# The last step of a recurrence: kept rows raised and loaded early, scale in the matrix, first turns on other banks

## The chip, the core and the metric

One core of a Trainium2 chip runs the whole program. The metric is device time in microseconds of one execution, the median of the runs shown; a profile of one execution comes with it. TensorE (PE) multiplies matrices; VectorE (DVE), ScalarE (ACT) and GpSimd (POOL) work on elements; SyncE (SP) issues transfers. In the profile PEld is TensorE's weight load, which overlaps its products.

## What is computed

Two layers, each a graph attention over 3327 nodes of 256 features and a feed-forward part. This document is about the end of layer 1: a layer norm, thirty steps of a small recurrence, and a residual.

```python
def step(h, _):
    h = h + 0.01 * jnp.tanh(h)
    h = h * jax.nn.sigmoid(h)
    h = _layernorm(h, ln_w, ln_b)
    h = jnp.einsum('bsc,dc->bsd', h, W) + b
    return (h, None)
x, _ = jax.lax.scan(step, x, None, length=N_ITERS)      # 30 steps
...
x = x + _L1_gnn_ref(_layernorm(x, axis=-1), adj, L1_gnn_W, L1_gnn_a)
x = x + _L1_ffn_ref((_layernorm(x, axis=-1))[None], L1_ffn_ln_w, L1_ffn_ln_b, L1_ffn_W, L1_ffn_b)[0]
```

The `x` of the last line's sum is needed thirty steps after it was last touched.

## The kernel before

The rows are 26 tiles of 128, held in SBUF as `x`. Layer 1's attention (`attend`) ends tile by tile; `begin_state` (L1070) writes the finished rows to `kept` in DRAM (L1072) and then normalizes `x` in place, times S = 100. So the recurrence's state lies in `x`, scaled by S, and the rows for the residual lie in `kept`.

`recurrence_parameters` (L845) prepares the step: `wc` is the weight matrix with the norm's weight in it, without its column mean, times S; `bb` is the bias, times S. `fb` holds the bias as loaded, over all partitions.

The 26 tiles form seven groups, six of four tiles and one of two. A number `at` runs over all groups of all steps: group `at % 7` of step `at // 7`, with `LAST` = 210. Each group goes through `tanh` (ACT, L1112), `add` (POOL, L1115), `silu` (ACT, L1119), `measure` (VectorE, L1124 and L1127), `invert` (POOL, L1132: the inverse deviation `rr`), a transposition, `product` (TensorE, L1181) and `evict` (VectorE, L1191: `x = po * rr + bb`). Transposition is done in one of two ways. Groups 1 and 3 (and group 0 of the first step) are turned on TensorE (`turn_here`, L1145) into PSUM banks, and ACT or VectorE copies them out (L1148). Groups 0, 2, 4, 5 and 6 go by DMA: ACT splits the words into halves (L1156), SP sends them to DRAM (`send_away`, L1158) and fetches them back transposed (`take_back`, L1168). The received tiles lie in slices of the space that held the adjacency matrix, which is why the profile calls them `adjT`.

The order is written out by hand. One loop over `at` calls the stages of different groups: tanh for group at + 6, invert for at + 1, send for at + 4, add for at + 5, product and evict for at, measure for at + 3, take_back or turn for at + 3. From the second step on (for TensorE from the third turn on) `keep_in_program_order` holds every engine's queue, SP's too, to that order. The earlier instructions, among them the first two groups' turns, are placed by a scheduler in between those of the attention before them.

PSUM has eight banks. Layer 1 uses two for single banks (`ps`) and six for its accumulators (`ps_o`, read at L1064 and L1065); the recurrence keeps `ps` and puts two more single banks (`ps_t`) and two double ones for its products where the six were. `turn_here` takes its banks from `ps` and `ps_t` by turns, `ps` first.

In the last step `evict` does more: it loads the group's rows from `kept` (L1198, on SP's queue, two buffers), adds them to 1/S times the result (L1199) and stores the sum through `move_pairs` (L74, SP's queue, L77). The last two tiles hold 255 rows; their store is three transfers, of 112 rows of pairs, 15 and a single row.

Of the kernel before, what the change touches and what calls it, by code (L numbers as in the profile page):

```python
# [11 lines left out]
F32 = mybir.dt.float32  # L12
# [5 lines left out]
ALU = mybir.AluOpType  # L18
# [3 lines left out]
P = 128  # L22
ALPHA = 0.2
EPS = 1e-5
N_STEPS = 30
S = 100.0
G = 4
# [4 lines left out]
def gat_moe_gat_recurrent_ffn(ctx: ExitStack, tc: tile.TileContext, a: dict, out: bass.AP):  # L32
    nc = tc.nc
    N, D = a["x"].shape
    KD = D // P
# [9 lines left out]
    groups = [range(t, min(t + G, NT)) for t in range(0, NT, G)]  # L45
# [9 lines left out]
    def spread(n):  # L55

        cut = n - n % 16
        return [r for r in ((0, cut), (cut, n)) if r[0] < r[1]]
# [14 lines left out]

    def move_pairs(dram, tile, c0, c1, into_dram):  # L74

        def move(dst, src):
            nc.sync.dma_start(*((dst, src) if into_dram else (src, dst)))  # L77

        full = min(c1, PAIRS - 1)
        if full > c0:  # L80
            move(
                dram[c0 * 2 * P : full * 2 * P, :].rearrange("(t p b) d -> p t (b d)", p=P, b=2),
                tile[:, : 2 * (full - c0), :].rearrange("p (t b) d -> p t (b d)", b=2),
            )
        if c1 == PAIRS:
            base, last = (PAIRS - 1) * 2 * P, 2 * (PAIRS - 1 - c0)
            for r0, r1 in spread(REST // 2):
                move(
                    dram[base + 2 * r0 : base + 2 * r1, :].rearrange("(p b) d -> p (b d)", b=2),
                    tile[r0:r1, last : last + 2, :].rearrange("p b d -> p (b d)"),  # L90
                )
            if REST % 2:
                move(dram[base + REST - 1 : base + REST, :], tile[REST // 2 : REST // 2 + 1, last, :])
# [262 lines left out]
    fb = rec.tile([P, D], F32, name="fb")  # L356
# [26 lines left out]
    with ExitStack() as moe:  # L383
# [21 lines left out]
        ps = moe.enter_context(tc.tile_pool(name="ps0", bufs=4, space=PSUM))  # L405
# [3 lines left out]
        def bank():  # L409
            return ps.tile([P, 512], F32, name="bank")  # L410
# [242 lines left out]
        for s0, n in ((0, FIRST), (FIRST, ALWAYS - FIRST)):  # L653
            no = 0
            for lane in range(SETS):
                here = two[:, 0, s0 + lane : s0 + n : SETS]
# [124 lines left out]
        def put(s, room, behind):  # L781
            planes = room.bitcast(I16)
            with tc.issue_after(behind):
                nc.scalar.copy(
                    planes.rearrange("p (b d) -> p b d", b=2),
                    gotten.pop(s).bitcast(I16).rearrange("p (d b) -> p b d", b=2),
                )
            put_down[s] = next(asked)
            nc.gpsimd.dma_start(put_down[s], planes)
# [55 lines left out]
        def recurrence_parameters(bank):  # L845


            pb = bank()[:, :D]
            for k in range(KD):
                nc.tensor.matmul(  # L850
                    pb, lhsT=lb[:, k : k + 1].to_broadcast([P, P]), rhs=fW[:, k, :], start=(k == 0), stop=(k == KD - 1)
                )
            nc.vector.tensor_tensor(bb, pb, fb, ALU.add)
            nc.vector.tensor_scalar(bb, bb, S, None, op0=ALU.mult)
            pc = bank()[:, :D]
            for k in range(KD):
                nc.vector.tensor_scalar(wc[:, k, :], fW[:, k, :], lw[:, k : k + 1], None, op0=ALU.mult)
                nc.tensor.matmul(pc, lhsT=ones_r, rhs=wc[:, k, :], start=(k == 0), stop=(k == KD - 1))
            for k in range(KD):
                nc.vector.scalar_tensor_tensor(wc[:, k, :], pc, -1.0 / D, wc[:, k, :], op0=ALU.mult, op1=ALU.add)  # L860
                nc.vector.tensor_scalar(wc[:, k, :], wc[:, k, :], S, None, op0=ALU.mult)
# [118 lines left out]
        wc = rec.tile([P, KD, D], F32, name="wc")  # L980
        bb = rec.tile([P, D], F32, name="bb")
# [18 lines left out]
    kept = dram.tile([NP, D], F32, name="kept")  # L1000
# [8 lines left out]
    ps = ctx.enter_context(tc.tile_pool(name="ps2", bufs=2, space=PSUM))  # L1009
# [72 lines left out]

    with ExitStack() as st:
        ps_t = st.enter_context(tc.tile_pool(name="ps3t", bufs=2, space=PSUM))
        turns = cycle((ps, ps_t))
        ps_o = st.enter_context(tc.tile_pool(name="ps3o", bufs=2, space=PSUM))
        last_p = st.enter_context(tc.tile_pool(name="last", bufs=2))

        apart = cycle([dram.tile([G * P, 2, D], I16, name=f"apart{q}") for q in range(4)])
        space = graph.tile([P, PAIRS, NP], BF16, name="adjT").rearrange("p c n -> p (c n)").bitcast(F32)  # L1090
        spaces = [space[:, i * G * D : (i + 1) * G * D] for i in range(8)]
        room_parts, room_back = cycle(spaces[:3]), cycle(spaces[3:])

        AWAY = (0, 2, 4, 5, 6)
        COUNT = len(groups)
        LAST = N_STEPS * COUNT

        class Group:

            def __init__(self, at):  # L1100
                self.at = at
                self.ts = groups[at % COUNT]
                self.n = len(self.ts)
                self.hs = x[:, self.ts[0] : self.ts[0] + self.n, :]
                self.away = at % COUNT in AWAY and at > 1

            def put(self, ins):
                return tc.keep_in_program_order(ins) if self.at >= COUNT else ins

# [25 lines left out]
                )  # L1135

            def turn_here(self):
                pool = next(turns)
                zT = steps["zT"].tile([P, G, KD, P], F32, name="zT")
                for c in range(self.n // 2):  # L1140
                    pt = pool.tile([P, 2, KD, P], F32, name="bank")
                    for j in range(2):
                        for k in range(KD):
                            (tc.keep_in_program_order if self.at > 1 else lambda ins: ins)(
                                nc.tensor.transpose(pt[:, j, k, :], self.z[:, 2 * c + j, k * P : (k + 1) * P], ident)  # L1145
                            )
                    copied = nc.vector.tensor_copy if (self.at % COUNT, c) == (3, 0) else nc.scalar.copy
                    self.put(copied(zT[:, 2 * c : 2 * c + 2, :, :], pt))  # L1148
                self.zT = lambda j, k: zT[:, j, k, :]
# [26 lines left out]
            def product(self):  # L1176
                self.po = ps_o.tile([P, G, D], F32, name="po")
                for j in range(self.n):
                    for k in range(KD):
                        tc.keep_in_program_order(  # L1180
                            nc.tensor.matmul(  # L1181
                                self.po[:, j, :], lhsT=self.zT(j, k), rhs=wc[:, k, :],
                                start=(k == 0), stop=(k == KD - 1),
                            )
                        )

            def evict(self):
                ts, n = self.ts, self.n
                for j in range(n):
                    self.put(  # L1190
                        nc.vector.scalar_tensor_tensor(  # L1191
                            self.hs[:, j, :], self.po[:, j, :], self.r[:, j : j + 1], bb, op0=ALU.mult, op1=ALU.add
                        )
                    )
                if self.at >= LAST - COUNT:
                    here = slice(ts[0] * P, (ts[-1] + 1) * P)
                    old = last_p.tile([P, G, D], F32, name="old")
                    nc.sync.dma_start(old[:, :n, :], kept[here, :].rearrange("(t p) d -> p t d", p=P))  # L1198
                    nc.vector.scalar_tensor_tensor(  # L1199
                        self.hs, self.hs, 1.0 / S, old[:, :n, :], op0=ALU.mult, op1=ALU.add  # L1200
                    )
                    move_pairs(out, self.hs, ts[0] // 2, (ts[-1] + 1) // 2, True)

        live = {}

        def on(at, *what):
            if 0 <= at < LAST:
                if at not in live:
                    live[at] = Group(at)
                for w in what:  # L1210
                    w(live[at])

        for at in range(-6, LAST):
            on(at + 6, Group.tanh)
            on(at + 1, Group.invert)
            on(at + 4, lambda g: g.away and g.send_away())
            on(at + 5, Group.add)
            on(at, Group.product, Group.evict)
            on(at + 3, Group.measure)
            on(at + 3, lambda g: g.away and g.take_back())  # L1220
            on(at + 5, Group.silu)
            on(at + 3, lambda g: g.away or g.turn_here())
            live.pop(at, None)
# [49 lines left out]
```

## Time and profile before

| | |
|---|---|
| median of 3 runs | 1819.82 us (1819.78 to 1823.14) |
| the profiled execution | 1820.76 us |
| its span, first to last instruction | 1819.0 us |
| mean granted TensorE clock | 0.995 |
| busy: PE, DVE, ACT, POOL | 1764.8, 1303.0, 1214.2, 916.2 us |
| recurrence (L1181): TensorE's products | 2144 on tiles by DMA, 976 on turned ones (each product counts as two) |
| one step in the middle | 24.2 us |

A row of the timeline reads: start and duration in us, engine, line, operation, output from input, how many, and in brackets the idle time before it with what ended it. The waits list who waited for whom, with the sum in us, the count and the longest. The table by stretch gives for each interval its length and the busy time of each engine with the number of instructions, then the granted clock (1.00 is full), the mean busy share of the DMA engines and GB/s. The landing of a transfer is read from the events of its semaphore in the trace.

### The profile page before, as it was taken

The page shows a single profiled execution, that of the slowest core. Times are in us where ns is not written, and L with a number is a line of the kernel's source. Part 1 is how long each engine was busy: PE and PEld are TensorE (multiplying, and loading weights), DVE is VectorE, ACT ScalarE, POOL GpSimd, SP SyncE. Part 2 cuts the span into 40 slices and gives each one's busy share as a digit, 9 for nine tenths or more (in the row PEclk, how much of TensorE's full clock was granted, in tenths as well). Part 3 has the DMA queues.
Part 4 walks back from the last instruction along what each step waited for, and adds up shares of the span by engine and source line. Part 5 has one row for each costly group of instructions (what it writes and reads, how often), then busy time and mean ns, then how long its engine had stood idle before and what let it go on. Part 6 is the DMA issues. An engine that isn't in the chain of part 4 may idle for free.

```text
span 1819.0 us, 32184 instructions
## 1 busy us (share of the span) xinstructions
PE 1764.8 (97%) x10768; PEld 1608.8 (88%) x10768; DVE 1303.0 (72%) x3861; ACT 1214.2 (67%) x1557; POOL 916.2 (50%) x702
## 2 busy tenths in 40 slices
PE   6999999999999999799999999999999999999997
PEld 6999999899999999688888878888888888888885
DVE  7888888863222222657677678889899988998997
ACT  2877677642212121456666579999999999999993
POOL 3011212155454542101111028999999999999993
PEclk9999999999999999899999999999999999999999
DMA  8996360247796875400000038888877888878778
GB/s 174 121 126 81 78 102 10 72 161 211 239 257 192 212 205 163 154 14 18 18 21 16 12 103 188 199 195 199 198 198 192 194 194 196 198 198 201 196 191 233
DMA packets 497026, 269.75 MB, mean 148 GB/s; under 512 B 361797, under 2 KB 469116, under 8 KB 496858
## 3 DMA queue, kind: packets, MB, share of 16 engines
q1 hardware_dynamic: 478722, 229.29, 50.6%
q0 software_dynamic: 13456, 33.60, 10.7%
q10 hardware_dynamic: 4680, 4.76, 0.8%
q8 instruction: 88, 1.44, 0.3%
q14 instruction: 80, 0.66, 0.1%
HBM read 168.19 MB, written 105.58 MB: 151 GB/s over the span
## 4 chain that ended last, share of the span: by engine, by line
PE 54%; DVE 3%; DMA 1%; issue 0%; ACT 0%; SPq 0%; POOL 0%; ACTq 0%; DVEq 0%; POOLq 0%
PE po L1181 36%; PE acc L286 15%; PE bank L1145 3%; DVE pT L281 1%; PE acc L163 1%; DMA old<-kept 1%; DVE x L1030 0%; DMA given<-wh,to 0%; DMA zT<-given 0%; DVE x L1199 0%; DVE x L1191 0%; DVE st L116 0%; POOL rstd L121 0%; DVE low L1064 0%; SPq L1168 0%
## 5 line engine op out<-in xcount | busy, mean ns | idle before, releaser
L276 ACT ACTIVATE e<-rb,minus,full 128x384 f32<-128x384 f32 (+3 forms) x494 | 399.3, 823 | 167.4 <-DVE pT L281 149.6
L1181 PE MATMUL po<-wc,adjT 128*128 128x256 f32 x2144 | 480.0, 380 | 7.5 <-DMA adjT<-apart 5.5
L1115 POOL TENSOR_TENSOR th<-th,x 128x1024 f32<-128x1024 f32 (+1 forms) x210 | 464.7, 2213 | 17.4 <-ACT th L1112 15.7
L281 DVE SCALAR_TENSOR_TENSOR pT<-e,part,adjT 128x384 f32<-128x384 f32 (+3 forms) x494 | 383.5, 782 | 118.4 <-PE acc L286 102.4
L1181 PEld LDWEIGHTS po<-wc,adjT 128*128 128x128 f32 x2144 | 405.9, 191 | 63.5 <-issue 4.9
L1191 DVE SCALAR_TENSOR_TENSOR x<-po,rr,bb 128x256 f32<-128x256 f32 x780 | 323.7, 476 | 73.4 <-PE po L1181 72.8
L286 PE MATMUL acc<-wh,pT 128*128 128x129 f32 x2704 | 310.4, 276 | 2.1 <-DVE pT L281 2.1
L286 PEld LDWEIGHTS acc<-wh,pT 128*128 128x128 f32 x2704 | 305.3, 192 | 2.9 <-DVE pT L281 2.7
L286 PE MATMUL acc<-s_wh,pT 128*128 128x257 f32 x1352 | 295.5, 381 | 4.0 <-DVE pT L281 4.0
L286 PEld LDWEIGHTS acc<-s_wh,pT 128*128 128x128 f32 x1352 | 255.8, 190 | 43.1 <-DVE pT L281 7.4
L1124 DVE BATCH_NORM_STATS2 stats<-z 128x6 f32<-128x256 f32 x780 | 274.4, 412 | 1.4 <-ACT z L1119 1.4
L1156 ACT COPY adjT<-z 128x1024 int16<-128x1024 int16 x268 | 266.9, 1039 | 2.1 <-DVE pT L281 2.0
L1132 POOL TENSOR_TENSOR rr<-v,neg_half 128x4 f32<-128x4 f32 (+1 forms) x210 | 205.6, 979 | 94.2 <-DVE v L1127 88.9
L121 POOL TENSOR_TENSOR rstd<-ve,neg_half 128x4 f32<-128x4 f32 (+3 forms) x28 | 31.9, 1141 | 409.4 <-DVE ve L119 325.6
L1112 ACT ACTIVATE th<-x 128x1024 f32<-128x1024 f32 (+1 forms) x210 | 208.8, 994 | 41.5 <-DVE x L1191 37.7
L1181 PE MATMUL po<-wc,zT 128*128 128x256 f32 x976 | 220.8, 379 | 0.1
L1119 ACT ACTIVATE z<-th 128x1024 f32<-128x1024 f32 (+1 forms) x210 | 209.0, 995 | 6.5 <-POOL th L1115 6.4
L1181 PEld LDWEIGHTS po<-wc,zT 128*128 128x128 f32 x976 | 182.9, 190 | 24.0 <-DVE x L1191 0.5
L931 ACT ACTIVATE e<-bank 128x512 f32<-128x512 f32 x61 | 36.4, 597 | 239.0 <-issue 184.8
L939 DVE TENSOR_TENSOR pT<-e,bank 128x512 f32<-128x512 f32 x61 | 41.9, 687 | 180.3 <-PE bank L881 160.1
L903 POOL DMA_INDIRECT given<-wh,to x61 | 61.1, 1001 | 114.5 <-DVE wh L902 100.0
L594 POOL DMA_INDIRECT lists<-pair,ati x52 | 63.1, 1214 | 107.8 <-DVE ati L581 50.0
(204 smaller groups left out, 1648.0 us busy)
## 6 DMA issues: line engine op xcount, KB each, us to landing
apart<-adjT SPq DMA_DIRECT2D x268, 256.0 KB
wh<-in_w_dram SPq DMA_DIRECT2D x120, 512.0 KB
first_set<-in_w_dram SPq DMA_DIRECT2D x63, 512.0 KB
in_bytes<-in_adj_dram POOLq DMA_DIRECT2D x3, 2496.0 KB
asked<-e POOLq DMA_DIRECT2D x42, 128.0 KB
adjT<-apart SPq DMA_TRANSPOSE x268
x<-in_x_dram SPq DMA_DIRECT2D x6, 512.0 KB
kept<-x SPq DMA_DIRECT2D x8, 384.0 KB
```

Of the source, the lines that this page charges most:

```text
L276: nc.scalar.activation(e[:, : n * P], rb[:, : n * P], AF.Relu, scale=sc.full[:, j, h : h + 1], bias=sc.minus[:, j, h : h + 1],)
L281: masked = nc.vector.scalar_tensor_tensor(pT[:, : n * P], e[:, : n * P], sc.part[:, j, h : h + 1], adjT[:, j // 2, ts[0] * P : (ts[-1] + 1 ...
L286: nc.tensor.matmul(po[c], lhsT=pT[:, c * P : (c + 1) * P], rhs=wh[:, j, h, :], start=(j == 0 and c % per_bank == 0), stop=(j == NT - 1), s ...
L594: put = nc.gpsimd.indirect_dma_start(out=lists, out_offset=bass.IndirectOffsetOnAxis(ap=ati[: rows(t), s, j : j + 1], axis=0), in_=pair[: ...
L1112: self.put(nc.scalar.activation(self.th, self.hs, AF.Tanh, scale=1.0 / S))
L1115: self.put(nc.gpsimd.tensor_tensor(self.th, self.th, self.hs, ALU.add))
L1119: self.put(nc.scalar.activation(self.z, self.th, AF.Silu, scale=1.0 / S))
L1124: self.put(nc.vector.bn_stats(stats[:, j, :6], self.z[:, j, :]))
L1132: nc.gpsimd.tensor_tensor(self.r[:, : self.n], self.v[:, : self.n, 1], neg_half[:, : self.n], ALU.pow)
L1156: self.put(nc.scalar.copy(parts[:, c : c + 2], halves[:, c : c + 2]))
L1181: nc.tensor.matmul(self.po[:, j, :], lhsT=self.zT(j, k), rhs=wc[:, k, :], start=(k == 0), stop=(k == KD - 1),)
L1191: nc.vector.scalar_tensor_tensor(self.hs[:, j, :], self.po[:, j, :], self.r[:, j : j + 1], bb, op0=ALU.mult, op1=ALU.add)
```

## The change

The kept rows get the bias added while they lie in DRAM: seven accumulating DMAs from GpSimd (`raise_old`), one for each group, after the product and eviction of group g in step 2 + 2g. Seven loads on SP's queue (`load_old`) bring the raised rows into SBUF, that of group g in step 16 + g, into seven slices of the old adjacency space. A second matrix `wc_last` = `wc` / S is made with the first load, and the last step's products use it. The last step's eviction is then `x = po * rr + old` and nothing more. For stores `move_pairs` takes SP's and ACT's queue by turns, beginning with SP in each call. The bias without S now stays in `fb`. The first two turns take their banks from `ps`, later ones from `ps_t` and `ps` by turns.

```diff
     def move_pairs(dram, tile, c0, c1, into_dram):
+        queues = cycle((nc.sync, nc.scalar) if into_dram else (nc.sync,))
         def move(dst, src):
-            nc.sync.dma_start(*((dst, src) if into_dram else (src, dst)))
+            next(queues).dma_start(*((dst, src) if into_dram else (src, dst)))
...
-            nc.vector.tensor_tensor(bb, pb, fb, ALU.add)
-            nc.vector.tensor_scalar(bb, bb, S, None, op0=ALU.mult)
+            nc.vector.tensor_tensor(fb, pb, fb, ALU.add)
+            nc.vector.tensor_scalar(bb, fb, S, None, op0=ALU.mult)
...
-        turns = cycle((ps, ps_t))
+        turns = cycle((ps_t, ps))
-        last_p = st.enter_context(tc.tile_pool(name="last", bufs=2))
...
+        wc_last = spaces[8][:, : KD * D].rearrange("p (k d) -> p k d", k=KD)
+        olds = [
+            spaces[9 + i].rearrange("p (t d) -> p t d", d=D)[:, : len(ts), :] for i, ts in enumerate(groups)
+        ]
...
             def turn_here(self):
-                pool = next(turns)
+                pool = next(turns) if self.at > 1 else ps
...
-                                self.po[:, j, :], lhsT=self.zT(j, k), rhs=wc[:, k, :],
+                                self.po[:, j, :], lhsT=self.zT(j, k), rhs=(wc if self.at < LAST - COUNT else wc_last)[:, k, :],
...
-                            self.hs[:, j, :], self.po[:, j, :], self.r[:, j : j + 1], bb, op0=ALU.mult, op1=ALU.add
+                            self.hs[:, j, :], self.po[:, j, :], self.r[:, j : j + 1],
+                            olds[self.at % COUNT][:, j, :] if last else bb, op0=ALU.mult, op1=ALU.add,
                         )
                     )
-                if self.at >= LAST - COUNT:
-                    here = slice(ts[0] * P, (ts[-1] + 1) * P)
-                    old = last_p.tile([P, G, D], F32, name="old")
-                    nc.sync.dma_start(old[:, :n, :], kept[here, :].rearrange("(t p) d -> p t d", p=P))
-                    nc.vector.scalar_tensor_tensor(
-                        self.hs, self.hs, 1.0 / S, old[:, :n, :], op0=ALU.mult, op1=ALU.add
-                    )
+                if last:
                     move_pairs(out, self.hs, ts[0] // 2, (ts[-1] + 1) // 2, True)
+
+            def rows_kept(self):
+                return kept[self.ts[0] * P : (self.ts[-1] + 1) * P, :].rearrange("(t p) d -> p t d", p=P)
+
+            def raise_old(self):
+                bias = fb[:, None, :].to_broadcast([P, self.n, D])
+                tc.keep_in_program_order(nc.gpsimd.dma_start(self.rows_kept(), bias, accum_op=ALU.add))
+
+            def load_old(self):
+                if self.at % COUNT == 0:
+                    for k in range(KD):
+                        self.put(nc.vector.tensor_scalar(wc_last[:, k, :], wc[:, k, :], 1.0 / S, None, op0=ALU.mult))
+                tc.keep_in_program_order(nc.sync.dma_start(olds[self.at % COUNT], self.rows_kept()))
...
             on(at, Group.product, Group.evict)
+            if at // COUNT == 2 + 2 * (at % COUNT):
+                on(at, Group.raise_old)
+            if at // COUNT == N_STEPS // 2 + 1 + at % COUNT:
+                on(at, Group.load_old)
```

More of the change, by code (lines that the diff above doesn't have):

```diff
@@ L1084, in gat_moe_gat_recurrent_ffn @@
         ps_t = st.enter_context(tc.tile_pool(name="ps3t", bufs=2, space=PSUM))
-        turns = cycle((ps, ps_t))
+        turns = cycle((ps_t, ps))
         ps_o = st.enter_context(tc.tile_pool(name="ps3o", bufs=2, space=PSUM))
-        last_p = st.enter_context(tc.tile_pool(name="last", bufs=2))
         apart = cycle([dram.tile([G * P, 2, D], I16, name=f"apart{q}") for q in range(4)])
         space = graph.tile([P, PAIRS, NP], BF16, name="adjT").rearrange("p c n -> p (c n)").bitcast(F32)
-        spaces = [space[:, i * G * D : (i + 1) * G * D] for i in range(8)]
-        room_parts, room_back = cycle(spaces[:3]), cycle(spaces[3:])
+        spaces = [space[:, i * G * D : (i + 1) * G * D] for i in range(9 + len(groups))]
+        room_parts, room_back = cycle(spaces[:3]), cycle(spaces[3:8])
         AWAY = (0, 2, 4, 5, 6)
         COUNT = len(groups)
+        wc_last = spaces[8][:, : KD * D].rearrange("p (k d) -> p k d", k=KD)
+        olds = [
+            spaces[9 + i].rearrange("p (t d) -> p t d", d=D)[:, : len(ts), :] for i, ts in enumerate(groups)
+        ]
         LAST = N_STEPS * COUNT
@@ L1187, in evict @@
             def evict(self):
-                ts, n = self.ts, self.n
-                for j in range(n):
+                ts, last = self.ts, self.at >= LAST - COUNT
+                for j in range(self.n):
                     self.put(
                         nc.vector.scalar_tensor_tensor(
-                            self.hs[:, j, :], self.po[:, j, :], self.r[:, j : j + 1], bb, op0=ALU.mult, op1=ALU.add
-                        )
-                    )
-                if self.at >= LAST - COUNT:
-                    here = slice(ts[0] * P, (ts[-1] + 1) * P)
-                    old = last_p.tile([P, G, D], F32, name="old")
-                    nc.sync.dma_start(old[:, :n, :], kept[here, :].rearrange("(t p) d -> p t d", p=P))
-                    nc.vector.scalar_tensor_tensor(
-                        self.hs, self.hs, 1.0 / S, old[:, :n, :], op0=ALU.mult, op1=ALU.add
-                    )
-                    move_pairs(out, self.hs, ts[0] // 2, (ts[-1] + 1) // 2, True)
+                            self.hs[:, j, :], self.po[:, j, :], self.r[:, j : j + 1],
+                            olds[self.at % COUNT][:, j, :] if last else bb, op0=ALU.mult, op1=ALU.add,
+                        )
+                    )
+                if last:
+                    move_pairs(out, self.hs, ts[0] // 2, (ts[-1] + 1) // 2, True)
+            def rows_kept(self):
[8 more added lines that the diff above has]
+                tc.keep_in_program_order(nc.sync.dma_start(olds[self.at % COUNT], self.rows_kept()))
         live = {}
```

## The prediction

> **What bounds the kernel now.** I read the page's busy times first, then the busy time by stretch, then the waits and the timeline of the last 35 us, then the turn from attention to recurrence. A steady step of the recurrence, beside the last stretch:
>
> ```profile
> core 0: us, PE busy (x) PEld busy (x) DVE busy (x) ACT busy (x) POOL busy (x), PEclk, DMA share, GB/s
> ...
> 1203.00:1227.20 24.20, 24.20 (x121) 21.28 (x120) 21.68 (x80) 22.70 (x27) 22.00 (x15) 1.00 0.89 198
> ...
> 1784.00:1819.00 35.00, 21.77 (x89) 17.32 (x88) 25.03 (x61) 5.64 (x7) 5.95 (x6) 0.90 0.89 243
> ```
>
> TensorE is busy for all 24.20 us of a step, at the full clock; VectorE has 2.5 us to spare, POOL 2.2, ACT 1.5, the DMA engines about a tenth. So a microsecond off another engine is worth nothing there, and a stall of TensorE costs its full length. In the last stretch TensorE works 21.77 us of 35. The waits there say why:
>
> ```profile
> PE po L1181 <- DMA adjT<-apart: 5.5, 2, 4.0
> DVE x L1199 <- DMA old<-kept: 5.5, 3, 2.2
> ...
> PE po L1181 <- DVE x L1199: 1.9, 1, 1.9
> ```
>
> Columns: who waited for whom, us in all, times, the longest. The last step loads the kept rows (`old`), stores results and fetches transposed tiles on one queue, and TensorE pays for each. In the timeline:
>
> ```profile
> 1791.11 3.72 PE L1181 MATMUL po<-wc,zT 128*128 128x256 f32 x16
> ...
> 1796.73 3.69 PE L1181 MATMUL po<-wc,adjT 128*128 128x256 f32 x16 [1.90 <-DVE x L1199]
> ...
> 1804.46 5.38 PE L1181 MATMUL po<-wc,adjT 128*128 128x256 f32 x16 [4.04 <-DMA adjT<-apart]
> ...
> 1811.34 1.97 PE L1181 MATMUL po<-wc,adjT 128*128 128x256 f32 x8 [1.50 <-DMA adjT<-apart]
> ...
> 1814.85 0.69 DVE L1199 SCALAR_TENSOR_TENSOR x<-x,old 128x512 f32<-128x512 f32 x1
> ```
>
> And at the start of the recurrence, the second group's turn (L1145) waits until layer 1's accumulators are read (L1065):
>
> ```profile
> 1062.99 11.54 PE L286 MATMUL acc<-s_wh,pT 128*128 128x257 f32 x52 [0.61 <-DVE pT L281]
> 1076.35 1.06 PE L1145 MATMUL bank<-ident,z 128*128 128x128 f32 x8 [1.82 <-DVE high L1065]
> 1077.25 3.62 PE L1181 MATMUL po<-wc,zT 128*128 128x256 f32 x16
> ```
>
> **The tail (removed: seven L1198 loads, seven L1199 additions).** L1199 is 2.27 + 5 x 1.23 + 0.69 = 9.1 us of VectorE, now folded into L1191, which reads the rows instead of `bb` at the same shape (0.41 us each, no change). The 1/S goes into `wc_last`, so the products cost the same. What would TensorE do without the waits? The last step's group 1 starts at 1783.94 and each group of four takes 3.454 us (17.27 for five in the chain of waits). Groups 1 to 5 end at 1801.2, the last half group at 1802.95, its eviction (0.1 + 0.87) at 1803.9. Now the last VectorE instruction ends at 1815.54: at most 11.6 us.
>
> Not all of that comes, because the stores stay, in the same queue, ahead of the transposes. In the built order of the changed kernel the store of group 1 stands before the transposes of group 4, that of 2 before those of 5, that of 3 before that of 6; each store waits for its eviction. Group 1's eviction ends near 1789.2, its store goes out at 1789.3 and the transposes at 1789.7, 0.4 later than in a steady step. How much a transfer delays what follows I take from the two stretches of the trace: in a steady step one send and two transposes take 5.8 us from issue to the last landing (1308.24 to 1314.04, by the DMA semaphores); with a load and a store of 512 KB between them 9.4 us (1795.75 to 1805.17). That is 3.6 us for two, 1.8 us each, of which about 0.5 is SP's issue (L1198's 492 ns). Against it stands the lead of the transposes: in the step at 1300 group 4's land 1.25 to 1.45 us before TensorE needs them, group 5's 0.95, group 6's 1.2, the next step's group 0's 1.7, group 2's 3.6. So in the tail about 0.45 us at group 4 and 1 at group 5, 1.5 in all (0.5 to 2.7). Tail: 11.6 - 1.5 = **10.1 us** off.
>
> **Stores on two queues.** The cycle is made anew in each call of move_pairs, so only the second of the last group's three stores goes to ACT. In the trace these three issues take 0.35, 0.45 and 0.23 us, and the 15-row and 1-row stores land with the 112-row one (1817.86 to 1817.95). The Trainium skill (DMA: Bandwidth & Descriptors, *Issuing engines are not separate DMA queues*) speaks against more than that: all issuers share the 16 DMA engines, and a second one saves issue time alone. By the rule that is 0.45 us at most, by the landings 0.1; I take 0. ACT has nothing behind this store.
>
> **First turns on layer 1's own banks.** In the built order the second group's eight turns now stand inside the last attention block (TensorE stalls there 0.6 to 1.2 us at a time, which covers their 0.87 us), and so do its two copies on ACT, group 3's statistics on VectorE and group 5's silu. After attention group 0's product follows at once: it starts when L1065 has freed the banks, near 1076.3, not 1077.25. The first full turn of the next step, now at 1099.14, could come at 1076.3 + 21.6 = 1097.9, because five sends stand earlier and the two `old` loads that ran ahead at 1075 and 1082 (4.0 and 4.7 us to landing) are gone: 1.2 us. The moved ACT work (2.2 us) may push the attention's end by up to 1 us. I take **0.9 us** off (0.2 to 1.3).
>
> **Loads in mid-recurrence (seven, steps 16 to 22).** SP's queue has each behind its group's sends and ahead of the next transposes. At 1.8 us of delay against the leads above: group 1's load 0.85, 2's 0.85, 3's 0.6, 4's 0.1; those of 0, 5 and 6 fall where the leads are long or the engines idle (1302.7 to 1304.8, 1320.6 to 1322.4). 2.4 us if all of it stands; if the engines take the bytes in their free tenth, 0 to 0.5. I take **2.0 us** lost.
>
> **Accumulating DMAs (seven, every other step from 2).** Two costs. On POOL the issue stands behind an L1115 and ahead of an L1132 and the next L1115, which silu (ACT), the sends and the transposes wait for in turn. The nearest rows are the plain POOL issues: 575 ns for 128 rows of 1 KB (L789), 742 for L325's 768 rows. With 512 rows I take 0.8 us, inside POOL's 2.2 us of slack and the transposes' 0.95 us of lead: nothing, and up to 0.8 each without that cover. The Trainium skill (SBUF — State Buffer, *A bandwidth-pool intuition that's wrong*) warns of another price: a GpSimd DMA of 0.62 us took 3.1 beside a VectorE copy, because its descriptors could not be written. By that 7 x (3.1 - 2.2) = 6 us would be lost; but a step here has one such copy, 0.65 us long and out of PSUM, and I go by the row. On the DMA engines no row shows an accumulation. Below: a plain 512 KB without SP's issue, 1.3 us. Above: source, destination and write one after the other, about 4 us. The destination is read as well, so I take 2.0. By POOL's times raise 0, 1 and 6 go out near idle DMA stretches; 2, 3, 4, 5 meet the leads 0.95, 1.2, 1.5, 2.0: 1.05 + 0.8 + 0.5 + 0 = **2.3 us** lost (0.4 to 10). A gain is excluded: it is added traffic.
>
> **The rest costs nothing.** Two VectorE scalings (0.41 us each by L128) under 2.5 us of slack, once; `fb` in place of `bb` at L853, same count.
>
> **Sum.** 1819.0 - 10.1 - 0.9 + 2.0 + 2.3 = 1812.3 us of span. The profiled execution took 1820.76, 1.8 above its span; the median, 1819.82, is 0.8 above it. So 1813.1, about **1813 us**.
>
> **The rivals.** A measurement of this kernel tells 0.2% (3.6 us) from no change.
> - *A, as summed*: 1808 to 1816. For it: 11.6 us of idle TensorE with named causes. Chance 0.66.
> - *B, a wait in place of the one removed*: the stores alone keep the transposes late. If groups 5 and 6 still wait 5.5 us on `apart`, the tail yields 6, and 1819.0 - 6 - 0.9 + 4.3 + 0.8 = 1817. For it: the DMA share is 0.89 in the tail. Against it: half of the extra bytes leave. Chance 0.22, with accumulations somewhat dearer than I put them.
> - *C, slower*: the accumulations block the engines, as read, read, write. With a delay of d us each, raises 0 to 5 cost about 6d - 9.7, since raises 0 and 1 then outlast their idle stretch too. The gain is gone at d = 3.1, 0.2% is lost at 3.7; with 4.5 it is 1819.0 - 11.0 + 2.0 + 17.4 + 0.8 = 1828. Chance 0.12.
>
> The range reaches from the best of A to the upper end of B: 1808 to 1822.
>
> **What would show it.** Right: no L1199; the last step's TensorE waits on `apart` below 3 us; the end about 10 us after group 5's start; group 0's product near 1076.3; steps 0 to 29 at 24.2 us except some of steps 2 to 14 and 16 to 22, up to 1 us longer. Wrong: steps with an accumulation 2 us or more longer (C), waits on `apart` of 4 us or more in the tail (B), or an attention that ends a microsecond later. Steps with no stretching at all would put the time near 1809.

## The result and the profile after

| | median, us | runs | ratio to the kernel before, 95% interval |
|---|---|---|---|
| before, same chip | 1820.51 (1819.13 to 1825.31) | 7 | |
| after | 1830.29 (1826.36 to 1835.36) | 7 | 1.0046 [1.0031, 1.0061] |

Slower, by about 8 to 10 us, where 7 us of gain were forecast. The profiled execution took 1833.43 us, with a span of 1831.7 at a clock of 0.993. Three microseconds of its distance to before lie ahead of anything that the change touches: the first kept rows were stored at 820.35 us, in the profile of before at 817.06. So I count from that store on: 1001.94 us before, 1011.35 after, +9.4.

A turn is a transposition on TensorE. I count a step from the turn of group 3 to the next one; the first of these is the first full turn below, and the tail runs from the last of them to the end. The table by stretch, of after: the step of group 0's accumulation, a quiet step, the step of group 4's accumulation, a part of it, and the tail.

```profile
core 0: us, PE busy (x) PEld busy (x) DVE busy (x) ACT busy (x) POOL busy (x), PEclk, DMA share, GB/s
1132.08:1158.22 26.14, 24.56 (x122) 21.25 (x121) 21.84 (x79) 23.84 (x28) 23.39 (x16) 1.00 1.05 204
1158.22:1182.42 24.20, 24.20 (x122) 21.42 (x121) 21.84 (x79) 22.09 (x26) 22.03 (x15) 1.00 0.87 195
1335.67:1366.68 31.01, 27.24 (x122) 23.31 (x120) 21.84 (x79) 25.32 (x29) 26.31 (x18) 0.89 0.96 177
...
1359.21:1366.03 6.82, 5.69 (x14) 4.55 (x15) 0.51 (x5) 3.28 (x4) 4.30 (x3) 0.50 0.82 156
...
1804.56:1831.70 27.14, 20.75 (x97) 17.16 (x95) 17.12 (x55) 6.58 (x8) 6.90 (x7) 0.97 0.85 229
```

The quiet step is as long as before. The tail has gone from 35.98 to 27.15 us. With an accumulation TensorE has the same 122 instructions in a longer step, and the DMA engines' share rises from 0.87 to 1.05 and 0.96. A share above 1 shows that the packets' times overlap, so that 1 less the share is not free room. In group 4's step the rate falls too (177 GB/s, 195 in the quiet step), in group 0's it doesn't. The waits of the recurrence in after (who for whom: us in all, times, longest) name the loser:

```profile
PE po L1185 <- DMA adjT<-apart: 12.3, 12, 3.8
...
PEld po L1185 <- DMA adjT<-apart: 3.6, 2, 2.9
```

Before, TensorE waited for these transposes twice in the whole recurrence, 5.5 us, and both waits were in the tail. One place in full, from the timeline of after:

```profile
1349.31 4.78 SPq L1172 DMA_TRANSPOSE adjT<-apart  x3
...
1350.37 1.28 POOL L1208 DMA_DIRECT2D kept<-fb  x1
...
1351.90 2.84 POOL L1119 TENSOR_TENSOR th<-th,x 128x1024 f32<-128x1024 f32 x1
...
1354.68 1.89 PE L1185 MATMUL po<-wc,adjT 128*128 128x256 f32 x8
...
1360.34 6.50 PE L1185 MATMUL po<-wc,adjT 128*128 128x256 f32 x16 [3.77 <-DMA adjT<-apart]
```

SP issued its transposes on time, at 1350.79 and 1352.12. By their semaphores they landed 9.41 and 9.94 us later, where 3.3 to 4.1 is usual (the step at 1300 of before), and the accumulation 10.99 us after its issue. TensorE waits 3.77 us for the first. The second, which lands at 1362.07, holds nothing up: the 16 products shown follow one another without a gap. They take 6.50 us, where 3.69 is usual, because the granted clock was 0.50 from 1359.21 to 1366.03 (the row of 6.82 us in the table). So 2.8 of the 6.81 us that this step lost come from the lower clock. It came with this wait, but what sets it off stays open here: in the kernel with all seven after group 4 (below) waits of 3.2 us passed at a clock of 1.00. What an accumulation costs its issuer and how long it is under way, from the rows of the tile `kept` in after:

```profile
L1208 POOL DMA_DIRECT2D kept<-fb x7: 1192/1297/1397, 1132.9 to 1461.1; - x7
...
DMA to landing us min/median/max: 5.9/7.4/11.0
```

(ns of the issue, least, median, most; then first and last start.) The last step of after, TensorE's rows of the timeline:

```profile
1812.35 3.62 PE L1185 MATMUL po<-adjT,zT 128*128 128x256 f32 x16
1816.85 3.69 PE L1185 MATMUL po<-adjT 128*128 128x256 f32 x16 [0.89 <-DMA adjT<-apart]
1821.30 3.69 PE L1185 MATMUL po<-adjT 128*128 128x256 f32 x16 [0.76 <-DMA adjT<-apart]
1825.24 1.97 PE L1185 MATMUL po<-adjT 128*128 128x256 f32 x8 [0.25 <-DMA adjT<-apart]
```

L1199's additions are gone, and of the waits on transposes (4.04 and 1.50) 1.9 us are left. The length of each step gives the whole account against the profile of before:

| term | predicted | after against before |
|---|---|---|
| tail, from the last full turn | -10.1 | -8.8 |
| start: first full turn, and first steps | -0.9 | -0.9 (-0.3; 0.6 us of longer first steps gone) |
| loads (steps 17 to 19: 24.62, 24.89, 25.15) | +2.0 | +2.1 |
| accumulations, groups 0 to 6: 1.94, 2.02, 3.28, 2.75, 6.81, 0.24, 0 | +2.3 | +17.0 (2.8 of it the lower clock) |
| sum | -6.7 | +9.4 |

The 0.24 falls in step 13, ahead of group 6's accumulation at 1461.13 us, so it stands under group 5; the expectation below has it under group 6. Three terms came out near their size and one was wrong by a factor of seven.

### The profile page after: what moved, and what is told of

Its sections match the earlier page's. It is cut to its first block, busy times and chain, and to the rows that moved or that the text cites. A ratio compares the mean times of both kernels' runs of the same rounds, so it can differ in the third digit from the quotient of the medians.

```text
span 1831.7 us, 32188 instructions
## 1 busy us (share of the span) xinstructions
PE 1771.9 (97%) x10768; PEld 1612.8 (88%) x10768; DVE 1296.7 (71%) x3856; ACT 1216.2 (66%) x1557; POOL 923.0 (50%) x709
## 3 DMA queue, kind: packets, MB, share of 16 engines
q0 software_dynamic: 16896, 37.01, 12.3%
## 4 chain that ended last, share of the span: by engine, by line
PE 52%; DMA 4%; DVE 2%; SPq 0%; issue 0%; ACT 0%; POOL 0%; DVEq 0%; ACTq 0%; POOLq 0%
PE po L1185 34%; PE acc L288 15%; DMA adjT<-apart 3%; PE bank L1149 3%; PE acc L165 1%; DVE pT L283 1%; DVE x L1032 0%; SPq L1172 0%; DVE x L1195 0%; DMA given<-wh,to 0%; DMA zT<-given 0%; POOL rstd L123 0%; DVE st L118 0%; ACT s_wh L1047 0%; DMA apart<-adjT 0%
## 5 line engine op out<-in xcount | busy, mean ns | idle before, releaser
L1119 POOL TENSOR_TENSOR th<-th,x 128x1024 f32<-128x1024 f32 (+1 forms) x210 | 472.7, 2251 | 13.9 <-ACT th L1116 12.3
L1185 PE MATMUL po<-wc,adjT 128*128 128x256 f32 x2072 | 466.1, 381 | 13.3 <-DMA adjT<-apart 10.4
L1185 PEld LDWEIGHTS po<-wc,adjT 128*128 128x128 f32 x2072 | 392.5, 191 | 69.9 <-DVE v L1131 5.9
L1195 DVE SCALAR_TENSOR_TENSOR x<-po,rr,bb 128x256 f32<-128x256 f32 x754 | 312.9, 476 | 90.1 <-PE po L1185 89.3
L1136 POOL TENSOR_TENSOR rr<-v,neg_half 128x4 f32<-128x4 f32 (+1 forms) x210 | 214.3, 1020 | 107.0 <-DVE v L1131 101.9
L1185 PE MATMUL po<-wc,zT 128*128 128x256 f32 x944 | 213.5, 379 | 1.8 <-DVE high L1067 1.8
L1185 PEld LDWEIGHTS po<-wc,zT 128*128 128x128 f32 x944 | 177.0, 190 | 25.0 <-issue 2.2
```

What stands on the lines that cost most here:

```text
L1119: self.put(nc.gpsimd.tensor_tensor(self.th, self.th, self.hs, ALU.add))
L1136: nc.gpsimd.tensor_tensor(self.r[:, : self.n], self.v[:, : self.n, 1], neg_half[:, : self.n], ALU.pow)
L1185: nc.tensor.matmul(self.po[:, j, :], lhsT=self.zT(j, k), rhs=(wc if self.at < LAST - COUNT else wc_last)[:, k, :], start=(k == 0), stop=(k ...
L1195: nc.vector.scalar_tensor_tensor(self.hs[:, j, :], self.po[:, j, :], self.r[:, j : j + 1], olds[self.at % COUNT][:, j, :] if last else bb, ...
```

## The experiments

My theory (D): an accumulation holds the DMA engines for longer than its bytes suggest, and the transposes behind it come late. Rivals: GpSimd is held by the issue (P); any GpSimd transfer of that size does it (S). In the first three kernels the bias is missing from the output. The runs come from several chips, on which the kernel before took 1821 to 1825 us; what compares is the ratio to it on the same chip.

**No accumulation.**

```diff
-            if at // COUNT == 2 + 2 * (at % COUNT):
-                on(at, Group.raise_old)
```

> The changed kernel without its seven accumulating DMAs; the rows are loaded as they are, so the bias is left out of the output. In the changed kernel's trace the steps with a raise are longer than 24.2 us by 1.95, 2.02, 3.28, 2.75, 6.81, 0 and 0.24 us, 17.0 in all; loads 2.1 longer, tail 8.8 shorter, start 0.6 shorter than before. Theory D (accumulation holds the DMA engines and makes transposes late) and theory P (POOL is held up by the issue) both expect all raised steps back at 24.2 us and about 1813 us, ratio 0.996 to before. If the loss lies elsewhere (the later attention end, the loads), it stays above 1820.

1820.14 us, ratio 0.9973 [0.9966, 0.9981], where 0.996 was forecast. Every step up to the loads took 24.2 us. The accumulations are the loss. Loads cost 2.3 us, and by group they are 0.76 (group 1), 0.83 (2), 0.64 (3), 0.10 (4) and nothing for 0, 5, 6. The trace's own sum, from the first kept store, is -7.1 us against before, more than the 4.9 of the ratio. The tail of before varies (35.98 here, 35.17 in the banks' run below), which leaves about 1.4 us that I can't place.

**A plain GpSimd transfer of the same rows, into another DRAM tensor.**

```diff
+        beside = dram.tile([NP, D], F32, name="beside")
...
-                tc.keep_in_program_order(nc.gpsimd.dma_start(self.rows_kept(), bias, accum_op=ALU.add))
+                tc.keep_in_program_order(
+                    nc.gpsimd.dma_start(
+                        beside[self.ts[0] * P : (self.ts[-1] + 1) * P, :].rearrange("(t p) d -> p t d", p=P), bias
+                    )
+                )
```

> The raises replaced by plain GpSimd DMAs of the same bias rows, same places, into another DRAM tensor (the bias is left out of the output). Theory D: a 1 KB row then holds an engine about 47 ns instead of 102, and nothing is read from DRAM; at most 0.5 us for each of those at groups 2, 3 and 4, 1 to 3 us in all, so 1813 to 1816. Theory S (any DMA that GpSimd issues costs this, by its descriptors and POOL's slower work after it): the raised steps stay 2 to 7 us longer, about 1830.

1822.59 us, 0.9986 [0.9972, 1.0]. The steps up to the loads stretch by 1.6 us in all, not 17: S falls. The size of the price stands in the rows of GpSimd's queue (packets, MB, share of 16 engines over the span). After:

```profile
q0 software_dynamic: 16896, 37.01, 12.3%
```

Without accumulations:

```profile
q0 software_dynamic: 13456, 33.60, 10.8%
```

Plain:

```profile
q0 software_dynamic: 14400, 37.01, 11.3%
```

Share times span: 225.3 us, 196.5, 205.6. The differences, 28.8 and 9.1, also carry the queue's other packets, which vary by up to 3 us from trace to trace. So I take these transfers' own packet records, averaged over the sixteen engines. The accumulations, six and a half of 512 KB, took 28.7 us, 4.4 us each; the plain transfers of the same bytes 9.9 us, 1.5 each. These are sums of packet times, and packets overlap. The comparison is impure: the plain transfer went in 832 packets of 4 KB, the accumulation in 3328 of 1 KB. A plain one in 1 KB packets was not run.

**An addition on GpSimd in the accumulation's place.**

```diff
+        beside = space[:, 16 * G * D : 17 * G * D].rearrange("p (t d) -> p t d", d=D)
...
-                tc.keep_in_program_order(nc.gpsimd.dma_start(self.rows_kept(), bias, accum_op=ALU.add))
+                tc.keep_in_program_order(nc.gpsimd.tensor_tensor(beside[:, : self.n, :], bias, bias, ALU.add))
```

> The raises replaced by an addition on POOL at the same places, of 128x1024 elements into an unused part of SBUF (the bias is left out of the output): about 2.4 us of POOL, as much as the issue (1.3) and the slower operations after it (0.46 each on two or three) together, and no DMA. Theory D: all steps near 24.2, at most 0.5 us longer, about 1813 to 1815. Theory P: 2 to 7 us for each step as in the changed kernel, about 1828.

1820.33 us, 0.9976 [0.9965, 0.9986]. The additions hold GpSimd for 1.9 us each, longer than the issue's 1.3, and stretch their steps by 0.3 us in all. That is less of GpSimd than the issue and its slower operations afterwards together; the next kernel has both in full.

**The same accumulations, all after group 5's product** (in steps 2, 4, ..., 14).

```diff
...
-            if at // COUNT == 2 + 2 * (at % COUNT):
-                on(at, Group.raise_old)
+            if at % COUNT == 5 and 2 <= at // COUNT <= 14 and at // COUNT % 2 == 0:
+                on(at, lambda g: raise_old(groups[at // COUNT // 2 - 1]))
```

> All seven raises issued after group 5's product in steps 2, 4, ... 14, where the changed kernel's trace showed no stretching; nothing else is changed. Theory D: there the DMA engines' idle stretch follows and only group 2's transposes, with 3.6 us of lead, come behind, so 0 to 0.5 us each, about 1814. Theory P: POOL's extra work is the same at every place, so 2 us and more each, above 1825.

1821.15 us, 0.9979 [0.9972, 0.9986], with the bias in the output again. The timeline of this kernel:

```profile
1344.28 1.26 POOL L1218 DMA_DIRECT2D kept<-fb  x1
...
1345.30 1.32 SPq L1162 DMA_DIRECT2D apart<-adjT  x2
...
1351.86 2.57 SPq L1172 DMA_TRANSPOSE adjT<-apart  x2
...
1355.70 3.69 PE L1185 MATMUL po<-wc,adjT 128*128 128x256 f32 x16 [0.44 <-DMA adjT<-apart]
```

The accumulation takes 8.05 us to land here too, but behind it stand only two sends, which landed 6.5 and 6.7 us after their issue; the next transposes go out at 1351.86 and land in 3.70. Four of seven accumulations cost nothing, the others 0.83, 0.68 (the one shown, with its wait of 0.44) and 0.69. That is 2.2 us in place of 17.0 with the same work on GpSimd, so P falls.

**The first turns' banks alone, on the kernel before.**

```diff
-        turns = cycle((ps, ps_t))
+        turns = cycle((ps_t, ps))
...
-                pool = next(turns)
+                pool = next(turns) if self.at > 1 else ps
```

> The kernel before with nothing changed but the choice of the PSUM banks for the turns. My theory (this part gives what the two traces show up to the first full turn, 0.6 us of recurrence): time within 0.1% of before, 0.9997; in the trace group 0's product starts about 1.3 us after the end of attention instead of 2.7, the first step is 24.2 us and not 24.5, and the stretch from the first kept row's store to the first full turn is 0.3 us shorter. Rival (the start gave the 0.9 us that I predicted, or more): that stretch is 0.9 us shorter or more. Rival (the moved turns lengthen the attention): that stretch is no shorter than before. The run also gives a second profile of stages that no variant touches: theory says that the 3 to 8 us by which the first kept row came later in the profiles of the changed kernels than in that of before vary from run to run, so this one may lie anywhere between 817 and 825 us; if the change slowed those stages, it lies at 817 again.

1824.12 us, 0.9993 [0.9984, 1.0002], which alone tells nothing from no change. The trace tells more. Group 0's product starts 1.8 us after the attention:

```profile
1080.79 3.69 PE L1181 MATMUL po<-wc,zT 128*128 128x256 f32 x16 [1.81 <-DVE high L1065]
```

The first full turn comes only 0.28 us earlier after the first kept store than before, because the attention ends 0.55 us later (258.02 us after that store, before 257.47). The first steps, 24.49 and twice 24.36 before, are all 24.2: 0.6 more, 0.9 in all. The expectation had overlooked the later two. That the banks shortened them is not shown: e10_one_queue has the same banks and steps of 24.47 and 24.36 again. The first kept store was at 820.96 us, though all code ahead of it is that of before: the 3 to 8 us there come and go from run to run.

**Whole rows: 4 KB per partition in one piece**, from a bias laid out four times.

```diff
-                tc.keep_in_program_order(nc.gpsimd.dma_start(self.rows_kept(), bias, accum_op=ALU.add))
+                tc.keep_in_program_order(
+                    nc.gpsimd.dma_start(
+                        kept[self.ts[0] * P : (self.ts[-1] + 1) * P, :].rearrange("(p t) d -> p (t d)", p=P),
+                        wide[:, : self.n * D], accum_op=ALU.add,
+                    )
+                )
...
+            if at == COUNT:
+                for j in range(G):
+                    tc.keep_in_program_order(nc.vector.tensor_copy(wide[:, j * D : (j + 1) * D], fb))
```

> The accumulating DMAs at their places, but each adds a bias laid out four times in SBUF to four whole rows of kept rows per partition, in one contiguous piece of 4 KB (two of 2 KB rows for the last group), in place of four separate rows of 1 KB. If the price is one for each packet (a read and a write that wait for each other), the packets become 4 KB, a raise takes 1.5 to 2.5 us of each engine instead of 4.0 to 5.4, and the raised steps stretch by 0 to 1 us each, some 4 in all: about 1821 where the changed kernel has 1834, ratio 0.998 to before. If the price is one for each byte, or if the chip cuts an accumulation into 1 KB packets anyway, a raise takes 4 us again and the time is that of the changed kernel, ratio 1.004 to 1.006.

1826.55 us, 1.0008 [1.0, 1.0016]: between the two forecasts. Its queue:

```profile
q0 software_dynamic: 14464, 37.01, 11.8%
```

By their own packet records the seven took 21.3 us, or 3.3 us for each 512 KB. So the packets did become larger (14464 in the queue in place of 16896), and a quarter of the price was the packets' (4.4 to 3.3); what is left is twice that of the plain transfer with packets of the same 4 KB (1.5). The steps stretched by 6.9 us, 3.84 of it at group 2, and not by 17. Of the 3.84, 1.8 came from products at a granted clock of 0.50 (1246.46 to 1249.87 us).

**All seven after group 4's product.**

```diff
...
-            if at // COUNT == 2 + 2 * (at % COUNT):
-                on(at, Group.raise_old)
+            if at % COUNT == 4 and 2 <= at // COUNT <= 14 and at // COUNT % 2 == 0:
+                on(at, lambda g: raise_old(groups[at // COUNT // 2 - 1]))
```

> All seven accumulating DMAs, of the same sizes and in the same seven steps, stand after group 4's product, where the changed kernel lost 6.8 us with its one raise; everything else as in the changed kernel. My theory (the place decides: behind it the transposes of groups 0 and 1 of the next step find the engines taken, and they have the least lead there): six raises of 6 to 7 us and one of 2 to 4, so 40 to 46 us of longer steps, about 1864 on a chip on which before takes 1825, ratio 1.019 to 1.023. Rival (6.8 was an outlier of one step, and a raise costs about 2.5 us wherever it meets a transpose): 16 us of longer steps, 1835, ratio 1.004 to 1.006.

1836.23 us, 1.0062 [1.004, 1.0083]. The rival was right: 3.4, 1.9, 3.4, 1.9, 4.3, 1.9 and 1.3 us, 18.1 in all. The 6.81 was an outlier. In the step that costs 4.3 here, the same step as in after, TensorE waits as long, in two pieces, but keeps the full clock (eight products in 1.97 and 1.99 us):

```profile
1359.27 1.97 PE L1185 MATMUL po<-wc,adjT 128*128 128x256 f32 x8 [2.75 <-DMA adjT<-apart]
1362.27 1.99 PE L1185 MATMUL po<-wc,adjT 128*128 128x256 f32 x8 [1.04 <-DMA adjT<-apart]
```

Why one accumulation costs 1.9 and the next 3.4 at the same place I don't know. The timeline of this kernel has a trap:

```profile
1144.98 4.86 SPq L1172 DMA_TRANSPOSE adjT<-apart  x3
...
1146.05 1.40 POOL L1218 DMA_DIRECT2D kept<-fb  x1
...
1155.02 0.38 DVE L1131 BATCH_NORM_AGGREGATE v<-stats 128x2 f32<-128x9 f32 x4
...
1155.42 2.83 PE L1185 MATMUL po<-wc,adjT 128*128 128x256 f32 x12 [3.17 <-DVE v L1131]
```

The bracket blames VectorE, whose last event happens to be close. But this product needs the transposed tile, and the transpose issued at 1146.71 landed at 1155.29, 0.13 us before TensorE went on: 8.58 us, against 4.44 at the same place without accumulations. The next took 7.99 against 4.11. So the delay that one accumulation puts on what follows is read here directly, at one place: 4.1 and 3.9 us.

**No accumulation, GpSimd adds the bias to the loaded rows; loads after group 5's product; stores of the last step behind the transposes.** This is the version that the experiments point to.

```diff
...
-                tc.keep_in_program_order(nc.gpsimd.dma_start(self.rows_kept(), bias, accum_op=ALU.add))
...
+            tc.keep_in_program_order(nc.gpsimd.tensor_tensor(olds[i], olds[i], bias, ALU.add))
...
+            if at % COUNT == 5 and N_STEPS // 2 + 2 <= at // COUNT < N_STEPS // 2 + 2 + COUNT:
+                on(at, lambda g: raise_old(at // COUNT - N_STEPS // 2 - 2))
+            if at % COUNT == 5 and N_STEPS // 2 + 1 <= at // COUNT < N_STEPS // 2 + 1 + COUNT:
+                on(at, lambda g: load_old(at // COUNT - N_STEPS // 2 - 1))
...
             on(at + 3, lambda g: g.away and g.take_back())
+            if at >= LAST - COUNT:
+                on(at, Group.store)
```

> No accumulating DMA: GpSimd adds the bias to the loaded rows in SBUF, a step after their load; the loads stand all after group 5's product, where the trace showed idle DMA engines, and each store of the last step stands behind the transposes of the third group on in SP's queue instead of ahead of them. The output is the reference's. Theory: loads 0 to 0.5 us (2.4 in the kernel without raises), additions 0 to 1, the tail from the last full turn 24.5 to 26 us (27.2 to 27.5 in the changed kernel, 36.0 before), start as in the changed kernel: about 11 us below before, less what the loads and additions cost, so a ratio of 0.994 to 0.996. Rival (the loads cost 2 us wherever they stand, for their bytes): a sum over the even steps of 2 us or more again, ratio 0.9965. Rival (the stores hold the transposes by their bytes and not by their place in the queue): the tail stays at 27 us.

1813.92 us, 0.9937 [0.9914, 0.9959]. Loads and additions together cost 1.2 us, more than the 0.5 of the loads alone that I had put, less than the rival's 2; the trace doesn't part the two. The tail is 25.53 us. Its TensorE:

```profile
1794.39 3.62 PE L1185 MATMUL po<-adjT,zT 128*128 128x256 f32 x16
1797.84 9.15 PE L1185 MATMUL po<-adjT 128*128 128x256 f32 x40
```

Groups 4, 5 and 6 run in one piece. Group 4's transposes go out 5.48 us after the last full turn, in after 6.76 us, because there SP stood at a store that waited for its eviction. The stores' bytes are the same, so it was their place in the queue.

**The accumulations early, right behind the storing of the kept rows**, nearly all during attention, and no addition on GpSimd; the rest as in the last kernel.

```diff
             normalized(tiles, tiles, S)
+            nc.gpsimd.dma_start(
+                kept[here, :].rearrange("(t p) d -> p t d", p=P),
+                fb[:, None, :].to_broadcast([P, len(ts), D]), accum_op=ALU.add,
+            )
...
```

> The kernel e8_pool_adds with the accumulating DMAs again in place of GpSimd's additions, but each issued right behind the storing of its kept rows, nine of them (eight of 384 KB, one of 256 KB), nearly all during layer 2's attention, where the DMA engines are 6 to 8% busy. The output is the reference's. Theory (an accumulation costs only where a transpose waits for the engines): no step of the recurrence stretches for them, at most the last one or two in the first step, so a ratio of 0.992 to 0.996, within a few us of e8_pool_adds. What the theory leaves open is read from the packets: if 1 KB packets of an accumulation still take 100 ns and more beside idle engines, that price is the accumulation's own; if they take about 50 ns, it came from the traffic of the recurrence. Rival (GpSimd held for 1.3 us and slower for 8 us afterwards hurts in the attention too, where it computes the factors of the normalization): the attention ends a microsecond or more later than 258.0 us after the first kept row's store.

1813.91 us, 0.9957 [0.994, 0.9974]. The recurrence is free of them but for the first step (25.49). The attention ends 259.38 us after the first kept store in place of 258.02: the rival's 1.4 us. TensorE's products and weight loads there wait 8.8 us for VectorE's `pT` in place of 6.6; how GpSimd's issue slows that chain I did not follow further. The rows of `kept` in this kernel:

```profile
L1078 POOL DMA_DIRECT2D kept<-fb x9: 1199/1285/1387, 822.2 to 1085.5; - x9
...
DMA to landing us min/median/max: 5.3/5.3/5.3
```

Beside DMA engines with a share of otherwise 0.05 to 0.08, an accumulation of 384 KB still takes 5.0 to 5.7 us to land, its 1 KB packets 123 to 137 ns each by the packet records (the recurrence's own 1 KB packets: about 50), 3.1 to 3.4 us of every engine. Most of the price is the accumulation's own, not the traffic's.

**The kernel of e8_pool_adds, all stores on SP's queue again.**

```diff
-        queues = cycle((nc.sync, nc.scalar) if into_dram else (nc.sync,))
+        queues = cycle((nc.sync,))
```

> The kernel e8_pool_adds with all stores of the last step on SP's queue again. The output is the reference's. Theory (the second queue is worth nothing, since only the middle one of the last group's three stores uses it): same time as e8_pool_adds within 0.2%, ratio 0.992 to 0.996, and the span from the last vector instruction to the end longer by 0 to 0.45 us. Rival (two queues save one issue and one completion): 0.5 us or more of that stretch.

1814.43 us, 0.9955 [0.9941, 0.997]. From the last vector instruction to the end 3.9 us, with two queues 4.1, one profile each. The second queue shows no gain.

## Why the prediction was wrong

- **Accumulations (+2.3 predicted, +17.0 measured): the step that failed**, in the words "The destination is read as well, so I take 2.0". I set bounds of 1.3 and about 4 us and picked a value between them without a row for it. The upper bound was near the truth: 4.4 us by the packets' times, 4.1 and 3.9 by the transposes' landing. That the transposes land late behind an accumulation is shown; how the engines share their time among the packets is not. The form of the sum (delay less lead) held for the whole, not for each place. Rival C's own formula, 6d - 9.7, gives 16.7 us with d = 4.4; its case of d = 4.5 stood 8.2 us above before, and the ratio says 8.4 (5.6 to 11.1). I gave that case 0.12. In detail, 4.4 less the leads gives 3.45 and 3.2 for groups 2 and 3 (3.28, 2.75 measured). "Near idle DMA stretches" meant stretches of 2.1 and 1.8 us: they swallowed a delay of 2.0, and of one of 4.4 they left 2.3 and 2.6 (measured 1.94 and 2.02). For group 4 the same sum gives 2.9: TensorE waited 3.8 and lost 2.8 more to the lower clock, for which the prediction had no term. For group 5 it gives 2.4, and 0.24 was measured. That C's formula meets 17.0 so closely is in part luck. And the DMA share of 0.89, read as a tenth to spare, says nothing of room: after has shares up to 1.05.
- **GpSimd's issue**: 1.3 us, not 0.8, and no cost of it shows (e4_raise_at_5), as predicted. The 3.1 us that the Trainium skill (SBUF — State Buffer, *A bandwidth-pool intuition that's wrong*) gives for a GpSimd transfer of 0.62 us beside a VectorE copy was not seen in the recurrence: the issues took 1.40 us at most.
- **Loads (+2.0)**: 2.1 in after, 2.3 in e1_no_raise, and there by group as predicted (0.85, 0.85, 0.6, 0.1 against 0.76, 0.83, 0.64, 0.10). This agreement by group is luck: the seven traces with the same loads give 1.8 to 3.4 us, and group 4's cost 0 in after and 1.1 in e3_pool_op and e7_raise_at_4. A delay less the leads gave the size of the sum, with a measured delay, and no more.
- **Start (-0.9)**: the number came out, the account for two thirds of it. At the prediction's own mark, the turn at 1099.14 in before, 0.6 was gained (0.3 up to the first full turn, 0.3 in step 0). The other 0.3 lie in longer steps 2 and 5 of before, which it doesn't name and which may vary from run to run (e10_one_queue).
- **Tail (-10.1)**: -8.8; against the 35.17 of e5_banks_alone -8.0. The stores' share of the 11.6 us was 2.8, not 1.5: the store of group 1 held group 4's transposes for 1.3 us, not 0.4. Moving them behind gave 1.6 to 1.7 back.
- **Two queues (0)**: e10_one_queue agrees.

Rival B, transposes kept late by the stores alone, was true only in small (1.9 us of waits).

## What to carry to other kernels

A transfer that an engine does not wait for still has a price wherever another transfer on the critical path stands behind it: estimate it as the delay that it was measured to cause less the lead of what follows, and put it where only transfers with a long lead follow. When the one unknown in such a sum has bounds that lie on both sides of the break-even point, the sign of the forecast is that unknown, and a middle value is no answer. Here the same bias came nearly free from an engine with slack.

## What the runs showed of the hardware

- An accumulating DMA from GpSimd of 512 KB took 4.4 us of packet time on each of the 16 engines in 1 KB pieces and 3.3 in 4 KB pieces; a plain one in 4 KB packets 1.5. It landed after 7.4 us in the median beside the recurrence's traffic.
- Its issue held GpSimd 1.3 us (plain 0.8; in 4 KB pieces 0.87), and GpSimd's own operations were slower behind it, for 10 us at group 4 of after: L1119 2.84 us in place of 2.37. Behind the plain transfer they were not.
- Beside the recurrence, whose quiet step has a DMA share of 0.87, it made the step 1.9 to 3.3 us longer for groups 0 to 3. Shares up to 1.05 show that packet times overlap.
- In after the granted clock was 0.50 for 6.8 us around the end of a wait of 3.77 us, and 16 products took 6.50 us in place of 3.69; before's tail shows the same behind its wait of 4.04 us (clock 0.50 from 1805.50 to 1808.90, 16 products in 5.38 us), e6_wide_rows behind one of 1.92 us, and in e7_raise_at_4 waits of 3.2 us passed without it.
